# Moving half of the first batch's v1 and v2 projections from the attention stage into the triangle stage, with another word order there

## The chip, the cores and the metric

The kernel runs on one core of one Trainium2 chip. The metric is the time of one execution on the device in microseconds (us); three runs of the kernel before gave 3804.72, 3806.33 and 3807.19 us, so its median is 3806.33 us. Everything is in float32. In what follows PE is the matrix engine, DVE the vector engine, ACT the scalar engine, POOL the GpSimd engine and SP the engine whose queue issues most of the transfers.

## The reference, cut to what matters

Two layers run one after the other on an input x of shape (4, 64, 64, 256): four batches of 4096 tokens with 256 channels. Layer 0 is plain attention over the 4096 tokens of a batch. Layer 1 is a "triangle" attention on the 64 x 64 grid of the same batch, followed by a small MLP.

```python
# layer 0, per batch, t = 4096 tokens
f, g, v = xt @ Wf, xt @ Wg, xt @ Wh            # 32, 32 and 128 channels
beta = softmax(g @ f.T, axis=-1)               # 4096 x 4096
y = xt + (beta @ v) @ Wo + bo                  # the input of layer 1

# layer 1, per batch, H = 8 heads of d_k = 32, N = 64
q, k, v1, v2 = y @ Wq, y @ Wk, y @ Wv1, y @ Wv2
scores = einsum('bilhd,bljhd->biljh', q, k) / sqrt(d_k)
att = softmax(scores, axis=2)                  # over l
out = einsum('biljh,bilhd,bljhd->bijhd', att, v1, v2)
h = layer_norm(y + out @ Wo)
out = layer_norm(relu(h @ W1 + b1) @ W2 + b2 + h)
```

The four projections q, k, v1 and v2 are all made from y, the result of layer 0. The heads are worked on in pairs: pair 0 and pair 1 use channels 0 to 127 of q, k, v1 and v2, pair 2 and pair 3 use channels 128 to 255.

## The kernel before, in the parts that the change touches

The program goes through the batches one by one. For each batch there is an attention stage (`layer0`) and then a triangle stage. Work of other batches that does not depend on the stage is woven into the triangle stages: the first one (`first_layer1`) carries the "front" of batches 1 to 3 (turning x, and making f, g and v of layer 0), the later ones carry the last part (output projection, norms, MLP) of the batch before.

The attention stage goes over eight blocks of 512 queries (`qb`), each in eight groups `k`. A group makes scores, exponentials and weighted values; between the groups stand the projections of the block before, from a table `parts`:

```python
def values(g): ...                             # L469: 4 matmuls of 128x512, o += v.T e
def scores(g): ...                             # L447: 4 matmuls of 128x512; ACT makes e = exp(s)

def proj(qb, name, m, ps=None, st=None, queue=nc.sync):     # q, k or v2; half m of the channels
    ps = pb("proj") if ps is None else ps
    for cc in range(2):
        nc.tensor.matmul(ps, w[:, cc, rows], y(qb, cc), start=(cc == 0), stop=(cc == 1))   # L526
    ...                                        # ACT copies it to st, a transfer stores it to DRAM

def proj1(qb, m, ps=None, st=None, queue=nc.sync):          # v1: all channels of half m of the tokens
    for n in range(2):
        for cc in range(2):
            nc.tensor.matmul(                  # L551, 128x256 each
                ps[:, ts(n, C)], y(qb, cc)[:, ts(m * 2 + n, P)], wv1_sb[:, cc, :],
                start=(cc == 0), stop=(cc == 1),
            )
    ...

parts = [
    [norm, bounds],
    [output],
    [lambda qb: proj(qb, "q", 0)],
    [lambda qb: proj(qb, "k", 0), lambda qb: proj(qb, "v2", 0)],
    [lambda qb: proj1(qb, 0)],
    [lambda qb: proj1(qb, 1), lambda qb: proj(qb, "q", 1)],
    [lambda qb: proj(qb, "k", 1)],
    [lambda qb: proj(qb, "v2", 1)],
]
...
for g in range(8 * NQB):
    ...
    if qb > 0 and not (qb == last and k >= 6):
        for part in parts[k]:
            part(qb - 1)
# ... then a tail: the projections of the last block, the scores of pair 0,
# and the first sums, weights and transposes of the triangle stage
```

The triangle stage has 32 steps, eight for each pair of heads. In each step eight products R = att x v2 of 128x2048 are made, `npool` of them on POOL (three, and two in every fourth step of the first batch) and the others on DVE; PE then contracts each with v1 in four matmuls:

```python
def product(self, step, m):                    # L849
    ...                                        # R: 3 buffers on DVE, Rp: 2 buffers on POOL
    eng.tensor_tensor(R, src.unsqueeze(1).to_broadcast([P, D, N]), v2[:, h], ALU.mult)

def accumulate(self, step, m):                 # L859
    for c in range(4):
        nc.tensor.matmul(acc[32 * c : 32 * c + 32, n % 2, :], w[:, n, c, 16 * h : 16 * h + 32], R[...], ...)
```

The front of a later batch comes in 24 pieces `s` (eight blocks for each of three batches). A piece reads 512 tokens of x into one buffer `xin`, turns them on PE, and the next piece is loaded into the same buffer once the turning is through:

```python
def load(self, s):                             # L329, buffer of its own: tag "hid", bufs=1
    self.x = work.tile([P, 4, C], F32, tag="hid", name="xin", bufs=1)
    nc.sync.dma_start(out=self.x, in_=xf[...])
def turned(self, s, cc): ...                   # word P: 4 transposes (L336)
def taken(self, s, cc): ...                    # word C: ACT copy, store
def values(self, s): ...                       # word v: 8 matmuls of 128x128 (L348); word u: copy, store
def factors(self, s): ...                      # word g: 16 matmuls with 32 columns (L239); word a: copy, store
```

The order of all this is a written list of words, `ORDER0`. It is gone through once for each period of four steps; `R23/1` is product 3 of step 2 of the period before, `A` an accumulation, `T` a taking of the sums, `S`, `W`, `t`, `c`, `V` the preparation of a step, `sp` and `e` the scores of the next pair. Every period had three front pieces:

```python
for period in range(NSTEP // 4 + 3):
    for word, late in words_of(ORDER0):
        i, last = period - late, int(word[-1])
        ...
        elif word[0] in "RATSWVtc":
            step_word(word[0], 4 * i + int(word[1]), last)
        else:
            front_word(word[0], 3 * i + int(word[1]), last)
```

Of the kernel before, what the change touches and what calls it, by code (L numbers as in the profile page):

```python
# [10 lines left out]
F32 = mybir.dt.float32  # L11
# [5 lines left out]
P = 128  # L17
# [3 lines left out]
N = 64  # L21
# [26 lines left out]

ORDER0 = """
    A22/1 t3/1 R23/1 V3/1 W0 A26/1 A21/1 g2/1 A23/1 A25/1 R24/1 T20/1 sp1/1 A24/1 S2 S3 c3/1 t0 R27/1
    v1/1 R31/1 R33/1 a2/1 A27/1 e11/1 e10/1 R30/1 A33/1 A31/1 R32/1 v2/1 u1/1 R37/1 P01 T21/1 A37/1
    A30/1 C01 S1 R35/1 c0 R36/1 A32/1 R34/1 P00 A35/1 A36/1 C00 g0 V0 R01 A34/1 u2/1 T30/1 R00 W1 R05
    T31/1 A05 R06 v0 A00 A01 V1 R03 R02 A03 t1 a0 c1 R04 u0 A06 R13 P11 R07 P10 A02 A07 R15 W2 R12 A04
    T00 C11 T01 sp0 R16 t2 e01 R10 c2 A12 P21 e00 R11 C10 S0/-1 A15 W3 A13 A16 C21 P20 A10 R17 R14 V2
    A11 A14 A17 R26 g1 R25 R20 T11 T10 a1 R22 R21 A20 C20
""".split()


# [1 line left out]
def attention_then_triangle_kernel(  # L62
# [23 lines left out]
    def pb(name):  # L86
        return psB.tile([P, 512], F32, tag="b", name=name)
# [303 lines left out]
                nc.sync.dma_start(out=F.yT[1], in_=d["x"][P : 2 * P, :])  # L391


    def layer0(b, F, safe, rest):
        yT, gT, fT = F.yT, F.gT, F.fT
        if safe:
            F.reduced()

# [122 lines left out]
        def proj(qb, name, m, ps=None, st=None, queue=nc.sync):  # L521
# [19 lines left out]
            else:  # L541
# [2 lines left out]
                    in_=st.rearrange("p (l j) -> p l j", j=N),  # L544
                )

        def proj1(qb, m, ps=None, st=None, queue=nc.sync):
            ps = pb("v1p") if ps is None else ps
            for n in range(2):
                for cc in range(2):  # L550
                    nc.tensor.matmul(  # L551
                        ps[:, ts(n, C)], y(qb, cc)[:, ts(m * 2 + n, P)], wv1_sb[:, cc, :],
                        start=(cc == 0), stop=(cc == 1),
                    )
# [9 lines left out]
        def proj_qk(qk, st):  # L564
# [33 lines left out]
            [lambda qb: proj(qb, "k", 1)],  # L598
            [lambda qb: proj(qb, "v2", 1)],
        ]  # L600
        last = NQB - 1
        scores(0)
        for g in range(8 * NQB):
            qb, k = divmod(g, 8)
            if b == 0 and not safe:
                for load in later[3 * g : 3 * g + 3]:
                    load()
                if g == 6:
                    fold_bias()
                if g == 20:  # L610
                    add_b2()
            if safe and k == 0 and qb + 1 < NQB:
                mx, todo = pieces(qb + 1)
                for qc, t in todo:
                    max_piece(qc, t, mx)
                row[qb + 1] = max_row(mx)
            if g + 1 < 8 * NQB:
                scores(g + 1)
            values(g)

            if qb > 0 and not (qb == last and k >= 6):
                for part in parts[k]:
                    part(qb - 1)
            if qb == last and k == 3:
                L.fetch_v1(0)
                L.fetch_v1(1)
            if qb == last and k == 5:
                if b > 0:
                    rest.load(NP * (b - 1))
                L.fetch_qk(0, True)  # L630
# [27 lines left out]
        def values1(m):  # L658
            proj1(last, m, None, stage[1][:, 1 + m, :], nc.scalar)
# [20 lines left out]
        hidden(0)  # L680
        score(3)
# [19 lines left out]
    class Layer1:  # L701
# [22 lines left out]
        def fetch_v2(self, pair, part=None):  # L724
            if part != 1:
                self.v2[pair] = big.tile([P, 2, D, N], F32, tag="v2", name="v2", bufs=2)
            v2 = self.v2[pair].rearrange("p h d j -> p (h d j)")
            l0, l1 = ((0, 56), (56, 64))[part] if part is not None else (0, 64)
# [419 lines left out]

    def step_words(L, fetched, stored):
        made, taken, sps = {}, {}, {}

        def do(w, step, m):
            if not 0 <= step < NSTEP:
                return
            if w == "R":
                if step not in made:
                    made[step] = 0
                    L.begin(step)  # L1160
                L.product(step, m)
                made[step] += 1
                if made[step] == 8:
                    if step == 1:
                        L.fetch_v2(1)
                    if step in (NIG - 1, 2 * NIG - 1):
# [36 lines left out]

        L.fetch_v1(2)
        return do, scores, take_scores
# [6 lines left out]
    def first_layer1(L, ahead, F):  # L1212
        turned = {}
        ahead.load(0)

        def fetched(step):
            if 24 <= step < 31:
                ahead.fetch(F, 1, step)

        step_word, scores, take_scores = step_words(L, fetched, lambda step: None)  # L1220

        def front_word(w, s, cc):
            if not 0 <= s < ahead.n:
                return
            if w == "P":
                ahead.turned(s, cc)
                turned[s] = turned.get(s, 0) + 1
                if turned[s] == 2:
                    ahead.load(s + 1)
                    if s + 1 == ahead.n:  # L1230
                        ahead.fetch(F, 1, 31)
            elif w == "C":
                ahead.taken(s, cc)
            elif w == "v":
                ahead.values(s)
            elif w == "u":
                ahead.valued(s)
            elif w == "g":
                ahead.factors(s)
            elif w == "a":  # L1240
                ahead.factored(s)

        for period in range(NSTEP // 4 + 3):
            for word, late in words_of(ORDER0):
                i, last = period - late, int(word[-1])
                if word[0:2] == "sp":
                    if i >= 0:
                        if i == last == 0:
                            scores(0)
                            for half in range(2):  # L1250
                                take_scores(0, half)
                        scores(2 * i + 1 + last)
                elif word[0] == "e":
                    if i >= 0:
                        take_scores(2 * i + 1 + int(word[1]), last)
# [178 lines left out]
```

## Time and profile before

| what | value |
|---|---|
| median of three runs | 3806.33 us |
| span of the profiled run | 3803.8 us |
| PE busy over the span | 97% |
| DVE, ACT, POOL busy over the span | 69%, 51%, 47% |
| mean granted PE clock | 0.990 |
| queue that SP, DVE and ACT transfers use: share of 16 engines | 29.2% |

The shares over the whole span mix stages. A stage is read from a stretch of the trace instead: in the first batch the attention stage lies at about 40 to 459 us, its tail at 459 to 497 us, the first triangle stage at 497 to 925 us, and the attention stage of the second batch begins at 925 us. A row of the profile names the line, the engine, the tiles (written on the left of the arrow, read on the right), how often, the busy time, the mean of one, and the idle time of the engine just before, with what ended it. The profile counts two PE instructions for most of the float32 matmuls written in the program.

### The profile page before, as it was taken

The numbers are of one execution on the slowest core, as the hardware profiler recorded it, in microseconds if no ns is written. First come the engines' busy times: TensorE is split into PE (matmuls) and PEld (weight loads), VectorE is DVE, ScalarE is ACT, GpSimd is POOL, SyncE is SP. The second block draws the span as 40 slices with busy tenths as digits, with TensorE's granted clock in tenths as the row PEclk, the third lists the DMA queues.
The fourth block names the chain that finished last, engine by engine and source line by source line (L and its number), as shares of the span: only waits on it lengthen the run. The fifth ranks groups of instructions, "written<-read, shape, count | busy, mean of one in ns | idle before, by whom it ended". The sixth has DMA issues, their size and how long they took to land.

```text
span 3803.8 us, 60205 instructions
## 1 busy us (share of the span) xinstructions
PE 3679.2 (97%) x23498; PEld 1797.3 (47%) x23498; DVE 2641.2 (69%) x2050; ACT 1931.2 (51%) x4257; POOL 1804.3 (47%) x930
## 2 busy tenths in 40 slices
PE   9999988998999999999999999999999999999997
PEld 5444444433444455554344455555344445555476
DVE  4444479997544459999544548999754445999976
ACT  3333355554333357776333346766533335677654
POOL 4000079996000049999200008999600004999944
PEclk9999999999999999999999999999999999999999
DMA  4111355544111164323111143343211116431221
GB/s 118 54 50 49 95 142 143 148 124 142 36 47 53 50 151 93 88 55 94 62 47 50 50 124 89 84 95 70 92 41 48 50 54 149 95 89 48 69 62 51
DMA packets 439750, 309.44 MB, mean 81 GB/s; under 512 B 299360, under 2 KB 404576, under 8 KB 432160
## 3 DMA queue, kind: packets, MB, share of 16 engines
q1 hardware_dynamic: 419952, 291.12, 29.2%
q10 hardware_dynamic: 16240, 8.59, 0.8%
q0 software_dynamic: 3264, 5.78, 0.7%
q8 instruction: 188, 3.08, 0.4%
q14 instruction: 106, 0.87, 0.1%
HBM read 165.88 MB, written 139.46 MB: 80 GB/s over the span
## 4 chain that ended last, share of the span: by engine, by line
PE 80%; POOL 5%; DMA 4%; DVE 4%; issue 4%; ACT 2%; SPq 1%; ACTq 0%; POOLq 0%; DVEq 0%
PE o L469 24%; PE acc L859 17%; PE proj L526 8%; PE s L447 7%; PE mp L1042 5%; PE zp L1062 5%; POOL Rp L849 4%; PE v1p L551 3%; PE sp L747 3%; DMA xin<-in_x_dram 2%; DVE R L849 2%; PE hp L918 2%; PE y L511 2%; PE att L801 1%; PE den L486 1%
## 5 line engine op out<-in xcount | busy, mean ns | idle before, releaser
L849 POOL TENSOR_TENSOR Rp<-attP,v 128x2048 f32<-128x2048 f32 x328 | 1490.1, 4576 | 448.4 <-DMA qk<-k 326.0
L849 DVE TENSOR_TENSOR R<-att,v 128x2048 f32<-128x2048 f32 x696 | 1546.9, 2274 | 103.5 <-PE acc L859 69.6
L476 DVE TENSOR_TENSOR esum<-esum,e 128x2048 f32<-128x2048 f32 x224 | 512.8, 2289 | 583.2 <-ACT e L458 579.6
L859 PE MATMUL acc<-R,wsel 128*32 128x512 f32 x5568 | 701.1, 602 | 24.6 <-DVE R L849 13.2
L458 ACT ACTIVATE e<-s 128x1024 f32<-128x1024 f32 x512 | 496.5, 1021 | 403.5 <-PE s L447 388.5
L970 POOL TENSOR_SCALAR nt<-mv 128x4 f32<-128x4 f32 (+1 forms) x51 | 9.9, 193 | 1287.2 <-DVE mv L935 1276.3
L469 PE MATMUL o<-e,vlo 128*128 128x512 f32 x1024 | 473.7, 605 | 0.0
L469 PE MATMUL o<-e,vhi 128*128 128x512 f32 x1024 | 472.6, 605 | 0.0
L859 PE MATMUL acc<-Rp,wsel 128*32 128x512 f32 x2624 | 351.0, 607 | 10.2 <-POOL Rp L849 9.2
L869 ACT COPY ao<-acc 128x1024 f32<-128x1024 f32 x256 | 254.1, 1020 | 186.7 <-PE acc L859 125.5
L859 PEld LDWEIGHTS acc<-R,wsel 128*32 128x32 f32 x5568 | 154.3, 110 | 356.5 <-issue 272.3
L469 PEld LDWEIGHTS o<-e,vlo 128*128 128x128 f32 x1024 | 184.0, 189 | 280.8 <-issue 280.8
L469 PEld LDWEIGHTS o<-e,vhi 128*128 128x128 f32 x1024 | 184.3, 189 | 279.7 <-issue 279.7
L447 PE MATMUL s<-gT,fT 32*128 32x512 f32 x2048 | 302.2, 640 | 4.7 <-ACT e L458 4.3
L784 ACT ACTIVATE es<-S,rd 128x64 f32<-128x64 f32 x1024 | 257.8, 336 | 2.1 <-ACT stage L538 1.3
L488 DVE RECIPROCAL rec<-den 128x512 f32<-128x512 f32 x32 | 107.5, 3358 | 215.6 <-PE den L486 215.6
L1062 PE MATMUL zp<-w,hid 128*128 128x256 f32 x1024 | 245.9, 385 | 7.5 <-ACT hid L1051 7.5
L1042 PE MATMUL mp<-hT,w 128*128 128x256 f32 x1024 | 249.5, 389 | 0.7 <-ACT hT L1014 0.7
L1042 PEld LDWEIGHTS mp<-hT,w 128*128 128x128 f32 x1024 | 186.5, 190 | 101.4 <-ACT attP L809 36.9
L1062 PEld LDWEIGHTS zp<-w,hid 128*128 128x128 f32 x1024 | 185.3, 190 | 72.1 <-issue 29.3
L538 ACT COPY st<-proj 128x512 f32<-128x512 f32 x104 | 60.9, 585 | 293.2 <-issue 165.9
L447 PEld LDWEIGHTS s<-gT,fT 32*128 32x128 f32 x2048 | 82.9, 182 | 193.6 <-issue 174.8
(166 smaller groups left out, 3833.6 us busy)
## 6 DMA issues: line engine op xcount, KB each, us to landing
v<-v2d SPq DMA_DIRECT2D x24, 1024.0 KB, 12.4
v1c<-v1d SPq DMA_DIRECT2D x128, 128.0 KB, 2.8
aT<-ao SPq DMA_DIRECT2D x1024, 16.0 KB, 1.9
A<-aT SPq DMA_DIRECT2D x256, 64.0 KB, 2.1
out_dram<-z SPq DMA_DIRECT2D x63, 256.0 KB, 2.5
y<-yT SPq DMA_DIRECT2D x56, 256.0 KB, 2.1
q<-st SPq DMA_DIRECT2D x56, 256.0 KB, 2.6
v1d<-st SPq DMA_DIRECT2D x56, 256.0 KB, 2.2
```

The costliest lines, as they stand in the source:

```text
L447: nc.tensor.matmul(s_ps[r // 2][:, r % 2, :], fT[rows, tt, ts(n, P)], gT[rows, ts(qb, QB)], start=True, stop=not safe,)
L458: nc.scalar.activation(e[g][:, 2 * j : 2 * j + 2, :], s_ps[j], AF.Exp)
L469: nc.tensor.matmul(o_ps[qb], F.v[tt][:, r * 4 + n, :], es[:, r, :], start=(k == 0 and r == 0), stop=(k == 7 and r == 3),)
L476: nc.vector.tensor_tensor(esum[qb], esum[qb], es, ALU.add)
L526: nc.tensor.matmul(ps, w[:, cc, rows], y(qb, cc), start=(cc == 0), stop=(cc == 1))
L551: nc.tensor.matmul(ps[:, ts(n, C)], y(qb, cc)[:, ts(m * 2 + n, P)], wv1_sb[:, cc, :], start=(cc == 0), stop=(cc == 1),)
L784: nc.scalar.mul(e[:, i, :], rows[:, i, :], rec[:, i : i + 1])
L849: eng.tensor_tensor(R, src.unsqueeze(1).to_broadcast([P, D, N]), v2[:, h], ALU.mult)
L859: nc.tensor.matmul(acc[32 * c : 32 * c + 32, n % 2, :], w[:, n, c, 16 * h : 16 * h + 32], R[:, ts(c, 8), :].rearrange("p d j -> p (d j)"), ...
L869: nc.scalar.copy(self.ao[step][:, ts(np, 2)].rearrange("p k d j -> p k (d j)"), self.acc[step][np])
L1042: nc.tensor.matmul(self.mp[:, fc % 2, :], w1_sb[:, cc, ts(fc, P)], self.hT[tt][:, cc, :], start=(cc == 0), stop=(cc == 1),)
L1062: nc.tensor.matmul(zp[:, n, :], self.hid[tt][:, fc, ts(n, P)], w2_sb[:, fc, :], start=(fc == 0), stop=(fc == 3 and tt not in self.hT2),)
```

## The change

One half of v2 and of v1 of batch 0, the channels 128 to 255 which only the pairs 2 and 3 read, is no longer made in the attention stage. It is made in the first triangle stage, in eight blocks, by a class `Late` with four new words: `m` makes v2 of a block and `n` copies and stores it, `o` makes v1 and `p` copies and stores it. `Late` reads y back from DRAM into two buffers. v2 of pair 2 is fetched from DRAM by rows as they get stored. To make room, the front pieces are spread two to a period over the first four periods and four to a period over the last four. ORDER0 is a new list throughout. The aim is to take PE work out of a stage in which PE is the busiest engine and to put it into one in which PE has idle time.

```diff
 ORDER0 = """
-    A22/1 t3/1 R23/1 V3/1 W0 A26/1 A21/1 g2/1 A23/1 A25/1 R24/1 T20/1 sp1/1 A24/1 S2 S3 c3/1 t0 R27/1
...  (five more lines)
+    A21/2 g1/2 S3/1 W1/1 A27/2 A23/2 A26/2 a1/2 V3/2 A24/2 P31/2 C21/2 R32/2 m1/2 T20/2 c3/2 P30/2 C31/2
+    t0/1 v2/2 n1/2 R25/2 A25/2 R33/2 sp0/1 T21/2 A32/2 C30/2 R34/2 R36/2 R30/2 A33/2 e00/1 u2/2 e01/1
+    o1/2 R31/2 g2/2 P00/1 c0/1 R37/2 A34/2 A36/2 A30/2 A31/2 A37/2 V0/1 R35/2 C00/1 T30/2 t1/1 R00/1
+    p1/2 P01/1 a2/2 C01/1 A35/2 R03/1 T31/2 A00/1 R02/1 g0/1 a0/1 R05/1 R07/1 A05/1 A03/1 v3/2 R06/1
+    u3/2 m0/1 S2/1 W2/1 c1/1 v0/1 V1/1 R01/1 A02/1 n0/1 R04/1 A07/1 A01/1 A04/1 R12/1 P11/1 u0/1 P10/1
...  (three more lines)
 """.split()
...
+    def v1_half(ps, ys, m):
+        for n in range(4):
+            for cc in range(2):
+                nc.tensor.matmul(
+                    ps[:, ts(n, P)], ys[cc][:, ts(n, P)], wv1_sb[:, cc, ts(m, P)],
+                    start=(cc == 0), stop=(cc == 1),
+                )
...
+    class Late:
...
+        def load(self, q):
+            self.y = []
+            for cc, tag in enumerate(("A", "yc")):
+                t = work.tile([P, 512], F32, tag=tag, name="yb", bufs=1)
+                nc.sync.dma_start(out=t, in_=self.io["y"][ts(cc, P), ts(q, 512)])
+                self.y.append(t)
...
+        def word(self, w, q):
...
+            if w == "m":
+                ps = self.ps[w, q] = pb("v2p")
+                for cc in range(2):
+                    nc.tensor.matmul(ps, wv2_sb[:, cc, ts(1, P)], self.y[cc], start=(cc == 0), stop=(cc == 1))
+                self.made(q)
+            elif w == "o":
+                ps = self.ps[w, q] = pb("v1p")
+                v1_half(ps, self.y, 1)
+                self.made(q)
+            else:
+                st = work.tile([P, 512], F32, tag="sx", name="sx", bufs=1)
...                                            # n: copy, store v2, fetch its rows; p: copy, store v1
+        def fetch(self):
+            if self.room and self.fetched < self.stored:
+                self.L.fetch_rows(2, 8 * self.fetched, 8 * self.stored)
+                self.fetched = self.stored
...  (layer0)
+        late = b == 0
...
+        if late:
+            parts[3] = [lambda qb: proj(qb, "k", 0)]
+            parts[4] = [lambda qb: proj(qb, "v2", 0)]
+            parts[5] = [proj1_half]
+            parts[6] = [lambda qb: proj(qb, "q", 1)]
+            parts[7] = [lambda qb: proj(qb, "k", 1)]
...
-            if qb > 0 and not (qb == last and k >= 6):
+            if qb > 0 and not (qb == last and k >= 6 + late):
...
-        proj(last - 1, "v2", 1, None, stage[0][:, 1, :])
+        if not late:
+            proj(last - 1, "v2", 1, None, stage[0][:, 1, :])
...
-        values1(0)
+        if late:
+            proj1_half(last, stage[1][:, 1, :], nc.scalar)
+        else:
+            values1(0)
...
-        values1(1)
+        if not late:
+            values1(1)
...
-        proj(last, "v2", 1, None, stage[2][:, 1, :], nc.scalar)
+        if not late:
+            proj(last, "v2", 1, None, stage[2][:, 1, :], nc.scalar)
...  (first_layer1; "sp" and "e" count the scores from 2 * i now, without a special first one)
+                elif word[0] in "mnop":
+                    if 0 <= i < 4:
+                        own.word(word[0], 2 * i + last)
+                elif 0 <= i < 4 and int(word[1]) < 2:
+                    front_word(word[0], 2 * i + int(word[1]), last)
+                elif 4 <= i < 8:
+                    front_word(word[0], 4 * i - 8 + int(word[1]), last)
-                else:
-                    front_word(word[0], 3 * i + int(word[1]), last)
```

More of the change, by code (lines that the diff above doesn't have):

```diff
@@ L51 @@
 ORDER0 = """
-    A22/1 t3/1 R23/1 V3/1 W0 A26/1 A21/1 g2/1 A23/1 A25/1 R24/1 T20/1 sp1/1 A24/1 S2 S3 c3/1 t0 R27/1
[L53 to L57, printed above, removed]
+    A21/2 g1/2 S3/1 W1/1 A27/2 A23/2 A26/2 a1/2 V3/2 A24/2 P31/2 C21/2 R32/2 m1/2 T20/2 c3/2 P30/2 C31/2
[3 more added lines that the diff above has]
+    u3/2 m0/1 S2/1 W2/1 c1/1 v0/1 V1/1 R01/1 A02/1 n0/1 R04/1 A07/1 A01/1 A04/1 R12/1 P11/1 u0/1 P10/1
+    A06/1 T00/1 sp1/1 C11/1 T01/1 R13/1 R15/1 R14/1 A13/1 e10/1 e11/1 t2/1 C10/1 R10/1 A12/1 R17/1 V2/1
+    A15/1 A14/1 A10/1 R16/1 R11/1 S0 R22/1 W3/1 g3/2 c2/1 W0 A17/1 R27/1 A11/1 v1/1 R20/1 a3/2 u1/1 o0/1
+    p0/1 S1 R21/1 T10/1 P20/1 t3/1 P21/1 A16/1 T11/1 C20/1 A20/1 R23/1 A22/1 R24/1 R26/1
 """.split()
@@ L391, in fetch, with store_v1 @@
                 nc.sync.dma_start(out=F.yT[1], in_=d["x"][P : 2 * P, :])
+    def v1_half(ps, ys, m):
[5 more added lines that the diff above has]
+                )
+    def store_v1(io, q, m, st, queue=nc.sync):
+        queue.dma_start(
+            out=io["v1"][ts(q, 512), ts(m, P)].rearrange("(n p) c -> p n c", p=P),
+            in_=st.rearrange("p (n c) -> p n c", n=4),
+        )
@@ new lines, in attention_then_triangle_kernel, with __init__, made @@
+    class Late:
+        def __init__(self, L):
+            self.L, self.io, self.q = L, L.io, None
+            self.ps, self.stored, self.fetched, self.room = {}, 0, 0, False
+            self.load(0)
+        def load(self, q):
[4 more added lines that the diff above has]
+                self.y.append(t)
+            self.used = 0
+        def made(self, q):
+            self.used += 1
+            if self.used == 2 and q + 1 < NQB:
+                self.load(q + 1)
+        def word(self, w, q):
+            if not 0 <= q < NQB:
+                return
+            if w == "m":
[9 more added lines that the diff above has]
+                st = work.tile([P, 512], F32, tag="sx", name="sx", bufs=1)
+                if w == "n":
+                    nc.scalar.copy(st, self.ps.pop(("m", q)))
+                    nc.sync.dma_start(
+                        out=self.io["v2"][ts(q, 8), ts(1, P), :].rearrange("l c j -> c l j"),
+                        in_=st.rearrange("p (l j) -> p l j", j=N),
+                    )
+                    self.stored = q + 1
+                    self.fetch()
+                else:
+                    nc.scalar.copy(st, self.ps.pop(("o", q)))
+                    store_v1(self.io, q, 1, st)
+        def fetch(self):
+            if self.room and self.fetched < self.stored:
+                self.L.fetch_rows(2, 8 * self.fetched, 8 * self.stored)
+                self.fetched = self.stored
@@ L545, in proj, with proj1_half @@
                 )
+        def proj1_half(qb, st=None, queue=nc.sync):
+            st, ps = staged(st), pb("v1p")
+            v1_half(ps, [y(qb, cc) for cc in range(2)], 0)
+            nc.scalar.copy(st, ps)
+            store_v1(io, qb, 0, st, queue)
         def proj1(qb, m, ps=None, st=None, queue=nc.sync):
@@ L670, in layer0 @@
             rest.affine_a(t0)
-        values1(0)
+        if late:
+            proj1_half(last, stage[1][:, 1, :], nc.scalar)
+        else:
+            values1(0)
         score(1)
@@ L726, in fetch_v2, with fetch_rows @@
                 self.v2[pair] = big.tile([P, 2, D, N], F32, tag="v2", name="v2", bufs=2)
+            if part != 2:
+                self.fetch_rows(pair, *(((0, 56), (56, 64))[part] if part is not None else (0, 64)))
+        def fetch_rows(self, pair, l0, l1):
             v2 = self.v2[pair].rearrange("p h d j -> p (h d j)")
-            l0, l1 = ((0, 56), (56, 64))[part] if part is not None else (0, 64)
             for i2 in range(2):
@@ L1145, in alone, with step_words @@
                 closed(n, known[n])
-    def step_words(L, fetched, stored):
+    def step_words(L, fetched, stored, late=None):
         made, taken, sps = {}, {}, {}
@@ L1165, in do @@
                         L.fetch_v2(1)
-                    if step in (NIG - 1, 2 * NIG - 1):
+                    if step == NIG - 1 and late is not None:
+                        L.fetch_v2(2, 2)
+                        late.room = True
+                        late.fetch()
+                    elif step in (NIG - 1, 2 * NIG - 1):
                         L.fetch_v2((step + 1) // NIG + 1)
@@ L1218, in fetched @@
                 ahead.fetch(F, 1, step)
-        step_word, scores, take_scores = step_words(L, fetched, lambda step: None)
+        own = Late(L)
+        step_word, scores, take_scores = step_words(L, fetched, lambda step: None, own)
         def front_word(w, s, cc):
@@ L1247, in first_layer1 @@
                     if i >= 0:
[L1248 to L1252, printed above, removed]
+                        scores(2 * i + last)
                 elif word[0] == "e":
                     if i >= 0:
-                        take_scores(2 * i + 1 + int(word[1]), last)
+                        take_scores(2 * i + int(word[1]), last)
                 elif word[0] in "RATSWVtc":
                     step_word(word[0], 4 * i + int(word[1]), last)
-                else:
-                    front_word(word[0], 3 * i + int(word[1]), last)
+                elif word[0] in "mnop":
[5 more added lines that the diff above has]
+                    front_word(word[0], 4 * i - 8 + int(word[1]), last)
         ahead.fetch(F, 1, NSTEP)
```

## The prediction, made before the changed kernel had run

> **What bounds the kernel now.** The whole-span shares (PE 97%) mix stages, so I first cut the span by windows into the stages of the first batch. Columns: length, then the busy time of PE, of its weight loads, of DVE, ACT and POOL, each with the number of instructions, the granted PE clock, the DMA share and GB/s.
>
> ```profile
> 40.00:459.00 419.00, 416.01 (x1353) 174.08 (x1352) 202.39 (x126) 156.38 (x183) 35.86 (x59) 1.00 0.21 60
> 459.00:497.00 38.00, 29.00 (x324) 16.79 (x324) 9.68 (x15) 16.70 (x32) 7.13 (x2) 0.91 0.79 189
> 497.00:925.00 428.00, 386.61 (x4284) 177.79 (x4284) 389.86 (x223) 232.62 (x610) 392.36 (x87) 0.96 0.52 138
> ```
>
> To be seen: in the attention stage (first line) PE is busy 416 of 419 us and everything else under half, so it is PE's stage and each us of PE work costs a us. In the triangle stage (third line) PE, DVE and POOL are all at 90 to 92%, none is full, and the PE clock is 0.96. So no engine bounds it throughout; something stops all three in turn. The waits of PE in that stretch say what:
>
> ```profile
> PE tp L336 <- DMA xin<-in_x_dram: 25.2, 7, 6.5
> PE acc L859 <- POOL Rp L849: 6.7, 14, 0.8
> PE acc L859 <- DVE R L849: 6.7, 7, 1.9
> ```
>
> (total us, times, longest.) The turning of x waits for its load, seven times, up to 6.5 us. PE runs in order, so nothing behind it goes on. The groups of DVE and POOL show the echo: their idle time ends when PE has released a product buffer.
>
> ```profile
> L849 DVE TENSOR_TENSOR R<-att,v 128x2048 f32<-128x2048 f32 x167 | 370.5, 2278 | 39.5 <-PE acc L859 35.0 <-DMA q<-stage 3.9 <-ACT attP L809 0.2
> L849 POOL TENSOR_TENSOR Rp<-attP,v 128x2048 f32<-128x2048 f32 x87 | 395.0, 4588 | 33.3 <-PE acc L859 32.7 <-POOL Rp L849 0.6
> ```
>
> Last I took the timeline of PE for the price of each piece of work. A single matmul's duration overlaps its neighbour's, so I use distances between starts:
>
> ```profile
> 428.26 1.88 PE L526 MATMUL proj<-yT,wk 128*128 128x512 f32 x4
> 429.98 1.88 PE L526 MATMUL proj<-yT,wv 128*128 128x512 f32 x4
> 431.79 1.14 PE L447 MATMUL s<-gT,fT 32*128 32x512 f32 x8
> 432.86 3.70 PE L469 MATMUL o<-e,vhi 128*128 128x512 f32 x8
> 436.40 1.89 PE L551 MATMUL v1p<-wv,yT 128*128 128x256 f32 x8
> 438.22 1.14 PE L447 MATMUL s<-gT,fT 32*128 32x512 f32 x8
> ...
> 911.48 2.05 PE L348 MATMUL vp<-wh,xT 128*128 128x128 f32 x16
> 913.58 1.06 PE L859 MATMUL acc<-Rp,wsel 128*32 128x512 f32 x8
> ```
>
> One v2 half of a block is 431.79 - 429.98 = 1.8 us, one v1 call 438.22 - 436.40 = 1.8 us (two calls to a block), and eight matmuls of 128x128 (the shape that the new v1 half has; vp, L348) some 2.0 to 2.1 us.
>
> **What the Trainium skill says.** "Perfetto Trace Analysis", section Identifying the Most-Contended Engine, warns that PE's busy share is no measure of distance to its limit, as pipelined matmuls overlap in the trace; the rows above agree (1.88 us of duration, 1.72 to 1.81 us from start to start), which is why I count by starts. The same page, section Optimization Strategy, recommends interleaving regimes whose busiest engine differs; that is what this change does, and the first two windows against the third show such regimes. "TensorE: Matmul & The Clock Gate", Part 1, says PE's clock is halved after about 3.4 us of idling and takes a similar time to come back. The trace fits: after a wait of 5.37 us the eight transposes of the next piece take 1.94 us, undisturbed ones 1.09 us, and the stage has a clock of 0.96 against 1.00 in attention. "DMA: Bandwidth & Descriptors", section Issuing engines are not separate DMA queues, says all transfers share the same 16 engines and interleave; the xin load lands after 6.5 us at the median, but the one issued at 607.36 us, right behind two 1 MB fetches of v2, held PE until 621.4 us, 14 us later.
>
> **The change, part by part.**
>
> *Out of the attention stage.* For each of the eight blocks v2's upper half goes (1.8 us) and the two v1 calls (3.6 us) become one of eight 128x128 matmuls (2.0 us): 1.8 + 1.6 = 3.4 us a block. In the loop lie six of the v2 halves (the last two are in the tail) and seven of the v1: 6 x 1.8 + 7 x 1.6 = 22 us, all of it on the path, as PE has no waits there. In the tail 2 x 1.8 + 1.6 = 5.2 us of PE work goes, but PE is busy only 29 of 38 us there and the first products wait for v2 by way of DRAM. I count 3 us. Sum: -25 us.
>
> *Into the triangle stage.* Eight times (1.8 + 2.0) = +30 us of PE, and sixteen ACT copies of 0.59 us, 9.4 us on an engine busy 233 of 428 us, which cost nothing. The work PE has there now, by starts: 256 accumulations x 0.88 = 225; weights' transposes 31 x 0.59 = 18; scores 12 x 1.85 = 22; 24 fronts of 1.0 (turning) + 0.9 (factors) + 2.0 (values) = 94. Together 359 us; then 389 us. DVE has 167 products 2.21 us apart plus 28 x 0.83 us of sums: 392 us. POOL has 89 products (two before the window) 4.55 us apart: 405 us. So PE comes up to the level of DVE, both a little under POOL, and POOL's 405 us is the floor of the stage. It takes 435 us now, from POOL's first product at 489.9 to 925.
>
> *The fronts.* A period is 53.5 us. With three pieces, the shortest stretch between the end of one turning and the next one in the old list (P10 to P21) held three or four accumulations, one score, one transpose and the rest of a front: about 6 us of PE work, less than the 6.5 us that the load takes. By the new list, half of the periods have two pieces, with P01 to P11 some 11.6 us apart (eight accumulations 7.0, factors 0.9, v2 1.8, values 2.0) and the other distances longer. In the four-piece periods the shortest is P21 to P31, eight accumulations and a front's factors, 8 us, and P01 to P11 9.9 us. All are over 6.5 us. In addition v2 of pair 2 is fetched by rows, in place of one 2 MB burst. I expect the 18.7 us of xin waits within the stage (25.2 less the 6.5 at its entry) to fall to about 5, from the one burst left (pair 3 is fetched in a four-piece period), and part of the slow-clock time with them. PE work of a period is then 28 + 2.4 + 3.7 + 15.6 = 50 us, beside 51 for DVE and 50 for POOL: with three engines this close, in order and with two or three product buffers, some new short waits must come. I put them at 4 us. So the triangle stage gets 14 - 4 = 10 us shorter.
>
> *Sum.* -25 - 10 = -35 us: 3806 - 35 = 3771 us; for small losses in the seam to the second batch (values and factors of the last front piece now stand behind the last accumulation, 3 us of PE) I say 3773 us.
>
> **The rivals.**
>
> *A: the stage is full, and the work only moves.* If the triangle stage now was limited by the coupling of three engines and not by xin, +30 us of PE lengthens it by up to 30 us, and the change gains nothing (3800 to 3810 us). For it: in the periods without an xin wait DVE and POOL are already busy 52 to 54 of 54 us. Against it: in those periods PE has only about 46 us of work, and in the triangle stage of the second batch, from 1425 to 1725 us, PE is busy 50 of 50 us in each slice with DVE and POOL at 48. So a list of words can hold three engines near full. A partial case, with the stage as long as before, gives 3806 - 25 = 3781 us.
>
> *B: the transfers become the wait.* Reading y back (4 MB), v1 stored in runs of 512 bytes, and stores of v2 followed at once by their fetch on the same SP queue could hold up the xin loads and the stores of the sums. For it: the DMA share is 0.52 here, and SP already waits in order on ACT. Against it: 8 MB of added traffic beside some 59 MB (138 GB/s x 428 us) is one seventh more, and y has 7 us or more of PE work to land in. This would put back the 14 us of xin gain or more: 3785 to 3795 us.
>
> *C: everything fits.* The triangle stage gets near POOL's floor, 405 / 0.97 = 417 us, 18 us shorter: 3806 - 25 - 18 = 3763 us, or a few us lower if the tail gains all its 5.2 us.
>
> **Range and chances.** The 22 us of the attention loop are nearly sure. The spread comes from the triangle stage: 18 us shorter (C) to 14 us longer (between A and B). That gives 3761 to 3795 us; with a margin below for a better clock, 3755 to 3795 us. To be faster by over 2% the time must be under 3730 us, 76 us less: that is more than the attention saving and all of the stage's idle time together (22 + 5 + 30), so 1%. Slower by over 2% needs the triangle stage 100 us longer, a broken list: 1%. Within 2%: 98%.
>
> **What would show it.** The seven loop blocks should be 22 us shorter together; if less, ACT or DVE limits attention. In the triangle stage the xin wait of PE should be under 12 us with its entry, the clock above 0.96, DVE and POOL busy 94% or more. A stage longer than 430 us with waits of PE on R and Rp speaks for A; waits on yb, xin or v2 from DRAM for B. The later batches should not change; if they do, my sum is wrong in a place I did not look at.

## The result, and the profile after

The changed kernel takes 3782.64 us (median of four runs, 3778.28 to 3790.86) against 3806.4 us before (3804.72 to 3807.19): a ratio of 0.9941, with a 95% interval of 0.9923 to 0.9958. The change gains about 24 us; 33 were forecast. The profiled runs span 3803.8 and 3782.1 us.

Stages by windows, the changed kernel (columns as before; the stages begin and end earlier now):

```profile
40.00:435.00 395.00, 393.40 (x1324) 161.35 (x1324) 201.00 (x125) 148.72 (x170) 35.95 (x59) 1.00 0.19 54
435.00:471.00 36.00, 25.55 (x370) 15.78 (x374) 10.27 (x14) 17.18 (x38) 6.98 (x2) 0.88 0.76 185
471.00:901.50 430.50, 398.85 (x4404) 199.32 (x4397) 391.54 (x225) 244.02 (x617) 393.11 (x87) 0.98 0.59 155
```

Attention is as full of PE as before, only shorter. The triangle stage has more PE work and a better clock (0.98 for 0.96), but DVE and POOL still only work 391 and 393 of 430 us. To compare two kernels I take marks that both have, from the timeline of PE, in us:

| mark | before | after | gained so far |
|---|---|---|---|
| last sum of the denominators of batch 1 (attention loop) | 454.41 | 431.80 | 22.6 |
| first transpose of the triangle stage | 487.67 | 461.82 | 25.9 |
| first scores of the second batch's attention | 925.00 | 901.48 | 23.5 |
| end of the span | 3803.8 | 3782.1 | 21.7 |

So the whole gain was there when the triangle stage began, and the stage went from 437.3 to 439.7 us.

The waits of PE in that stage, the changed kernel:

```profile
PE vp L352 <- ACT gf L251: 5.6, 2, 2.9
PE sp L844 <- DMA qk<-k: 5.6, 2, 4.6
PE v2p L439 <- DMA yb<-y: 5.3, 3, 4.5
PE tp L340 <- ACT gf L251: 4.1, 2, 2.4
PE tp L340 <- DMA xin<-in_x_dram: 3.9, 2, 2.8
PE vp L352 <- ACT xT L345: 3.0, 4, 1.0
```

The xin wait, 25.2 us before, is 3.9. In its place stand five others: the first scores wait for q and k at the entry, the late v2 for y, and the front's matmuls for a PSUM buffer that ACT empties late (the two rows with gf) or for ACT's copy of the turned x (xT).

All of PE's idle time in the stage fell by 10 us, from 47.7 to 37.7, and its busy time rose by 12 us, from 389.6 to 402.0, though the late matmuls alone take 31 us by distances between starts: the other matmuls together took less time than before, beside the better clock. Yet the stage is no shorter. The groups of DVE and POOL show the same:

```profile
L946 DVE TENSOR_TENSOR R<-att,v 128x2048 f32<-128x2048 f32 x168 | 374.1, 2276 | 40.0 <-PE acc L956 26.6 <-ACT attP L906 9.6 <-DMA q<-stage 3.8
L946 POOL TENSOR_TENSOR Rp<-attP,v 128x2048 f32<-128x2048 f32 x88 | 400.1, 4582 | 357.1 <-ACT attP L906 329.6 <-PE acc L956 17.4 <-ACT va L359 6.0
```

DVE's idle time is 40.0 us, as before (39.5), although POOL waits less on PE (17.4 for 32.7 us; the 329.6 is the attention stage before). To see when it idles I counted 21 DVE products at a time (a period's share) from the timeline and took the distance from start to start (the last has 20), in us:

| products | 1st | 2nd | 3rd | 4th | 5th | 6th | 7th | 8th |
|---|---|---|---|---|---|---|---|---|
| before | 65.5 | 50.6 | 57.4 | 50.4 | 56.3 | 49.5 | 52.5 | 49.5 |
| after | 60.0 | 51.3 | 51.1 | 57.8 | 55.7 | 51.2 | 53.5 | 50.0 |

The first three together are 11 us shorter, and two of them stand at DVE's own work of a period (21 x 2.21 + 4 x 0.83 = 50 us, and a few short waits). The other five are 10 us longer. The theory to test:

- **N (new waits).** Three things at definite places took back what the removed xin waits gave: the load of y around the change of pairs in the fourth period, the xin load behind the fetch of v2 of pair 3 in the fifth, and the one staging buffer of the factors in the periods with four fronts.
- **A (full stage).** The stage pays for the 30 us of PE work as such.
- **A2.** The transfers at the change of pairs hold the stage, and a wait that is taken away there comes back as another.

The load of y, PE and SP queue, the changed kernel:

```profile
652.76 1.95 PE L401 MATMUL v1p<-wv,yb 128*128 128x128 f32 x16
...
668.76 3.78 PE L439 MATMUL v2p<-yb,wv 128*128 128x512 f32 x4 [4.50 <-DMA yb<-y]
```

```profile
644.13 0.49 SPq L812 DMA_DIRECT2D qk<-q  x1
...
647.38 15.02 SPq L975 DMA_DIRECT2D aT<-ao  x8
...
664.35 0.87 SPq L424 DMA_DIRECT2D yb<-y  x2
```

The y buffers are free when the matmuls of 652.76 are through, at about 654.5 us. But the load is issued only at 664.35: ahead of it on SP are eight small stores whose issue took 15.0 us, behind 2 MB of q and k of the next pair. The same eight take 5.0 us elsewhere (at 665.79). PE waits 4.5 us, then works at a granted clock of 0.50 (3.78 us for four instructions that else take 1.98), and DVE idles 7.00 us until 677.58.

### The profile page after: what moved, and what is told of

It reads as the page before. It is cut to its first block, busy times and chain, and to the rows that moved or that the text cites. A ratio compares the mean times of both kernels' runs of the same rounds, so it can differ in the third digit from the quotient of the medians.

```text
span 3782.1 us, 60452 instructions
## 1 busy us (share of the span) xinstructions
PE 3667.2 (97%) x23626; PEld 1805.3 (48%) x23626; DVE 2642.4 (70%) x2050; ACT 1936.3 (51%) x4257; POOL 1806.1 (48%) x930
## 4 chain that ended last, share of the span: by engine, by line
PE 82%; POOL 7%; DMA 4%; DVE 3%; issue 2%; ACT 2%; SPq 1%; ACTq 0%; POOLq 0%; DVEq 0%
PE o L544 24%; PE acc L956 17%; PE proj L601 8%; PE s L522 7%; POOL Rp L946 5%; PE zp L1159 5%; PE mp L1139 5%; PE sp L844 3%; PE v1p L633 2%; PE hp L1015 2%; DMA qk<-k 2%; PE y L586 1%; DVE R L946 1%; PE att L898 1%; DMA xin<-in_x_dram 1%
## 5 line engine op out<-in xcount | busy, mean ns | idle before, releaser
L613 ACT COPY st<-proj 128x512 f32<-128x512 f32 x98 | 57.4, 586 | 288.3 <-PE proj L601 160.2
L854 ACT ACTIVATE S<-sp 128x512 f32<-128x512 f32 x128 | 129.9, 1119 | 93.7 <-PE sp L844 93.7
```

Source lines behind the costliest of these rows:

```text
L854: nc.scalar.activation(self.S[pair][:, :, l0 : l0 + 8].rearrange("p i l -> p l i"), sp[:, lh], AF.Copy if self.safe else AF.Exp,)
```

## The experiments

The time of each is the median of its own runs; intervals are of the ratio to the kernel before. "Stage" is from the first transpose to the first scores of the second batch in its one profiled run. One warning: the triangle and attention stages of the later batches, whose program text is the same in all kernels here, took between 2213.9 and 2221.2 us in the profiled runs (from the end of the stage to the last denominators of batch 4). A difference of some us in a total can therefore be chance; I read the stage first. The stage has a spread too, as single periods show whose text is the same: the first took 58.5 to 60.2 us in the changed kernel and in five of the runs below (e4, e6, e7, e9, e10), the eighth 50.0 in the changed kernel and 52.9 in e5. So a stage that differs by 3 us proves little; a period that comes out alike in several runs says more.

**The new order without the move** (e1).

```diff
-        late = b == 0
+        late = False
-        own = Late(L)          # and the words m, n, o, p do nothing
```

> The new word list and the uneven spread of the fronts, without the move: attention makes all of v1 and v2 as before. Theory N (new waits: the triangle stage kept its 437 to 440 us because one late load of y, the single staging buffer of the factors in the four-front periods and one late xin load took the place of the old xin waits): without the y loads the triangle stage should be some 8 to 10 us shorter than in the changed kernel, about 430 us from the first transposes to the attention of the second batch, and the whole 3806 - 7 = about 3799 us. Rival A (the stage is full and the moved 30 us of PE work is what it pays for): without this work the stage falls by 20 us or more, to 420 us or less, and the whole to about 3788 us.

3800.97 us, ratio 0.9989 (0.998 to 0.9998), stage 434.9 us. Nearer to N's 430 us than to A's 420: without the moved work the stage is only 4.8 us shorter than with it. It also says what the new list and spread alone are worth: 2.4 us of stage. The fourth period, with the change of pairs in it, takes 51.5 us here, for 57.8 in the changed kernel.

**The move without its PE work** (e2). This kernel leaves out the late matmuls of v1 and v2, so its output is not the reference's.

```diff
             if w == "m":
-                ps = self.ps[w, q] = pb("v2p")
-                ... matmuls
+                self.made(q)   # "o" likewise; n and p copy a weight tile in place of the result
```

> The changed kernel with the matmuls of the late v1 and v2 halves left out (30 us of PE work; wrong data is stored in their place, all copies, loads and stores stay). Attention is that of the changed kernel. Theory N: the periods 1 to 3 stay at 51.2 us, the DVE's own work, and only the wait for y (7 us of DVE idle in the period of the change of pairs) goes: 3773 to 3777 us. Rival A: the stage gets 20 to 30 us shorter: 3753 to 3763 us.

3779.95 us (3775.28 to 3780.9), ratio 0.9934 (0.9917 to 0.995), stage 434.5 us. The stage as a window, the changed kernel first, then this one:

```profile
461.80:901.50 439.70, 402.00 (x4451) 201.54 (x4452) 394.81 (x226) 248.65 (x636) 400.09 (x88) 0.98 0.60 158
463.60:898.10 434.50, 380.84 (x4288) 181.60 (x4288) 394.83 (x226) 248.06 (x636) 399.84 (x88) 0.96 0.59 159
```

**A falls**: leaving out 31 us of matmuls shortens the stage by 5 us, not by 20 to 30, and the second and third period stay at 51.4 and 50.7. PE's busy time falls by only 21 us, as the clock goes back to 0.96 and the other matmuls take 10 us longer. N's time is slightly missed, and for a reason: y is no longer waited for, but the periods around the change of pairs still take 55.8 and 56.7 us. DVE now waits there, in this kernel, for the stores:

```profile
681.26 6.68 DVE L941 TENSOR_TENSOR R<-att,v 128x2048 f32<-128x2048 f32 x3 [4.01 <-DMA aT<-ao]
...
703.81 4.49 DVE L941 TENSOR_TENSOR R<-att,v 128x2048 f32<-128x2048 f32 x2 [3.93 <-PE acc L951]
```

That is the first sign of A2. Set beside e1 it says more. Both kernels lack the late matmuls; e2 has the late loads of y, copies, stores and row fetches, and its fourth period takes 55.8 us for 51.5. The fetch of q and k for the next pair is in both. So the change of pairs alone does not cost the fourth period its time; most of it comes with the transfers and copies of the late work. The eight stores behind that fetch show it on SP, in e1:

```profile
673.69 9.36 SPq L975 DMA_DIRECT2D aT<-ao  x8
```

They are issued 1.5 us after the last fetch, as in the changed kernel, and take 9.4 us for its 15.0.

**The move with the old list** (e3).

```diff
-    ... the new list, 2 and 4 fronts to a period
+    ... t1 a0 c1 R04 u0 m0 A06 R13 P11 R07 n0 P10 ... C21 o0 P20 A10 p0 ...
+    ... a1 m1 R22 R21 A20 C20 n1   and   u1/1 o1/1 R37/1 p1/1 P01 ...   (the old list, 3 fronts)
```

> The move alone: the old word list with three fronts to each period, and the new words m, n, o, p put in at free places by hand. Theory N: the old xin waits stay (some 19 us within the stage) and 31 us of PE work come on top, in the first four periods, where PE then has 54 us of work against 51 of DVE: stage 445 to 455 us, the whole 3787 to 3800 us; so most of what the new list is worth, 5 to 15 us, shows here. Rival A: the same stage as in the changed kernel within 3 us, 3780 to 3785 us, as the work is the same.

3838.31 us, ratio 1.0087 (1.007 to 1.0103), stage 492.2 us: worse than either theory said, and slower than the kernel before. Its periods are 73, 66, 68, 70 and 59 us while the late work lasts, then 50 to 52. The waits of PE in its stage:

```profile
PE tp L338 <- DMA xin<-in_x_dram: 33.9, 6, 8.5
PE v2p L437 <- DMA yb<-y: 11.7, 2, 6.7
PE acc L954 <- DVE R L944: 7.8, 9, 1.9
```

I put the new words in by hand, so this is one bad placing and no bound on what the old list could carry. But the same work with the written list and the spread of the change takes 52 us less. PE's waits for xin and y alone are 45.6 us here and 9.2 there: whether the move pays at all depends on the order and the spread.

**An even spread** (e8), with the new list and the move.

```diff
-                elif 0 <= i < 4 and int(word[1]) < 2: ...      # two to a period, then four
-                elif 4 <= i < 8: ...
+                elif int(word[1]) < 3:
+                    front_word(word[0], 3 * i + int(word[1]), last)
```

> The changed kernel with three front pieces to each period in all eight periods, as before the change (and the word p1/2 moved ahead of P00/1, so that the two PSUM buffers suffice). PE then has some 54 us of work in the first four periods and 46 us in the last four, against 50 and 50. Theory N: the first four periods take 54 to 57 us in place of 51.2, the last four get at most 2 us shorter each: 5 to 15 us slower than the changed kernel, 3788 to 3798 us. Rival: PE's work does not bind at all, the spread is worth nothing: within 3 us of the changed kernel.

3795.8 us, ratio 0.9976 (0.9967 to 0.9984), stage 450.9 us. The time is the one that N said. The first five periods take 62.4, 56.9, 59.8, 57.8 and 60.7, where N said 54 to 57 for four of them, the last three 50.3, 50.3 and 46.0. The mechanism is at most partly the one expected: besides PE's sum of work, ACT stood for the one factor buffer, and this run does not part the two. In this kernel:

```profile
ACT gf L251 <- DMA ahf<-gf: 41.7, 7, 13.5
```

**The factor buffer** (e4, then e7 and e9). In the changed kernel ACT and SP show the wait:

```profile
801.16 0.37 ACT L251 ACTIVATE gf<-gf,bias_g 128x128 f32<-128x128 f32 x1 [6.81 <-DMA ahf<-gf]
```

```profile
794.04 0.61 SPq L370 DMA_DIRECT2D ahg<-gf  x1
794.74 0.43 SPq L370 DMA_DIRECT2D ahf<-gf  x1
```

The factors of one piece are stored from 794.0 us, behind a fetch of 512 KB and an xin load; those of the next piece can't be written before 801.2. PE's next values then wait 2.73 us for the PSUM buffer. First try:

```diff
-            t = work.tile([P, 2, C], F32, tag="h", name="gf", bufs=1)
+            t = work.tile([P, 2, C], F32, tag="sx" if s >= 8 and s % 2 else "h", name="gf", bufs=1)
```

> The changed kernel with a second staging buffer for the factors of every other front piece of the second half (the buffer that the late v1 and v2 copies no longer use). Theory N: the ACT waits for the store of the factors (16.7 us) go, and with them the 2 to 3 us that DVE and POOL lose in each of the last periods: 4 to 7 us faster than the changed kernel, 3776 to 3779 us. Rival A: no difference.

3780.64 us, ratio 0.9936 (0.992 to 0.9953), stage 441.6 us, the ACT wait 15.4 us for 16.7. Nothing, and the trace shows why: pieces 2 and 0 follow each other within 10 us in the list and are both even, so they still shared one buffer. So turns by the order of use:

```diff
+            self.turn = s >= 8 and not getattr(self, "turn", False)
+            t = work.tile([P, 2, C], F32, tag="sx" if self.turn else "h", name="gf", bufs=1)
```

> As the earlier run with a second factor buffer, which did nothing since the two pieces that follow each other within 10 us (a2 and a0 of the list) still had the same buffer: now the two buffers take turns by the order of use. Theory N: the ACT waits for the store of the factors (16.7 us) fall below 4 us and the last three periods lose 2 to 5 us together: 3777 to 3781 us. Rival A2: the waits go but the time stays, as POOL (50 us of work to a period) and DVE (51 us) take 51 us or more anyway: within 1 us of the changed kernel.

3781.0 us, ratio 0.9939 (0.9922 to 0.9956), stage 437.2 us. The wait for the store is gone and the last two periods fall from 53.5 and 50.0 to 52.8 and 46.4, but the fifth grows from 55.7 to 59.0. The borrowed buffer is still being stored from by the last late v1, in this kernel:

```profile
ACT gf L251 <- DMA v1d<-sx: 10.3, 1, 10.3
```

With the turns from piece 10 on (`s >= 10`):

> The factor buffers take turns as in the run before, but only from front piece 10 on, so that the second buffer is no longer shared with the last copies of the late v1 (that cost a wait of 10.3 us on ACT and a period of 59.0 in place of 55.7 us). Theory N: the stage falls by the 3 us of that wait to 434 us, the last three periods stay at those of the run before: 3775 to 3779 us. Rival A2 (the transfers at the change of pairs hold the stage, whatever buffer is doubled): within 1 us of the run before, 3780 to 3782 us.

3776.52 us (3775.52 to 3780.12), ratio 0.9921 (0.9907 to 0.9934), stage 434.4 us: that wait is gone too, the fifth period is at 56.0 again. N is right about this buffer. The stage is 5.3 us shorter, but 1.5 of that lie in the first period, whose text is the same; the last two periods give 4.0 us. The eighth takes 46.4 to 46.9 us in all five runs with the turns (e7, e9 to e12), for 50.0 in the changed kernel.

**The transfers at the change of pairs** (e5, e6, e10, e11). First, y on another queue, behind the copy of v1:

```diff
                     store_v1(self.io, q, 1, st)
+                    if q + 1 < NQB:
+                        self.load(q + 1, nc.scalar)     # in place of nc.sync, after the second use
```

> The changed kernel with the loads of y for the late halves issued on the ACT queue, right after the copy of v1 of the block before, in place of the SP queue, where the one for the last block stood behind 15 us of stores. Theory N (the single late y load costs 6 to 7 us of DVE and POOL idle at the change of pairs): the wait of PE for y goes, the stage gets 4 to 7 us shorter than the changed kernel's 439.7 us, the whole 3776 to 3779 us. Rival A2 (the run without the moved PE work still had 55.8 us and 56.7 us in the two periods around the change of pairs, so the transfers of that moment hold the stage anyway, through xin or the stores): the y wait goes but another takes its place, 0 to 2 us.

3795.06 us (3787.2 to 3799.87), ratio 0.997 (0.996 to 0.998), stage 450.5 us: both theories missed, it is 11 us worse. y's wait fell only from 5.3 to 3.5 us, and ACT could not empty the sums, since the stores of the sums were late, in this kernel:

```profile
ACT ao L960 <- DMA aT<-ao: 17.6, 3, 11.6
```

The fourth period takes 64.4 us. Why the stores were held so long by half a MB on the other queue I have not shown.

Second, v2 of pair 3 in pieces:

```diff
-                    elif step in (NIG - 1, 2 * NIG - 1):
-                        L.fetch_v2((step + 1) // NIG + 1)
+                    # at steps 15 to 21: 8 rows of each half of v2 of pair 3 (16 at step 21)
+                        L.fetch_rows(3, 8 * k, 8 * k + 8)
```

> The changed kernel with v2 of pair 3 fetched in seven pieces over seven steps in place of one 2 MB fetch. Theory N: the xin load behind that fetch lands in 7 us in place of 13, its wait of 2.8 us goes, and the period with 55.7 us gets 2 to 4 us shorter: 3778 to 3781 us. Rival A2: no difference.

3781.64 us, ratio 0.9939 (0.9923 to 0.9956), stage 442.1 us. PE's xin wait in the stage falls from 3.9 to 0.8 us and the fifth period from 55.7 to 52.5, as N says; then the 6th to 8th grow from 154.7 to 160.8 us together, with longer waits for the factor buffer (19.8 for 16.7 us). Of these 6 us 2.5 lie in the eighth, which took 52.9 in e4 and e5 too and can be chance. So the two cures belong together:

> The same with v2 of pair 3 fetched in seven pieces, which took the xin wait away before (2.9 to 0.8 us) but gave the gain back through longer waits for the store of the factors. Theory N: with two factor buffers those waits are gone, so the 3 us stay gained: 3772 to 3777 us. Rival A2: the pieces delay other stores, within 1 us of the run without them.

**3771.53 us** (3770.24 to 3775.67), ratio 0.9909 (0.9896 to 0.9923), stage 432.9 us: the fastest version here, 11 us below the changed kernel. Its stage accounts for 6.8 us of the 11. The rest lies before the stage (1.3) and in the later batches, where the text is the same, and I can't tell it from chance. Against e9 the fifth period gives 3.6 us, but the stage only 1.6. The fifth period is 52.5, the last two 54.4 and 46.9; only the entry (59.2) and the fourth period (57.5) are still long.

Third, to get y ahead of q and k, the words o0 and p0 moved forward (on e9):

```diff
-    ... A07/1 A01/1 A04/1 R12/1 P11/1 u0/1 P10/1 ... u1/1 o0/1 p0/1 S1
+    ... A07/1 o0/1 A01/1 A04/1 u0/1 R12/1 P11/1 p0/1 P10/1 ... u1/1 S1
```

> Factor buffers in turns from piece 10 on, and the words o0 and p0 moved forward by some 60 places, ahead of the fetch of q and k of the next pair, so that y of the next block is asked for before that 2 MB fetch and the stores behind it. Theory N (the y load is late because it stands behind the fetch): the wait for y at the change of pairs goes, the period of 57 us becomes 52 to 54 us: 3771 to 3776 us. Rival A2 (bandwidth at that moment is short, as y on the ACT queue showed, where the stores of the sums waited instead): y is no longer waited for, but the stage stays within 2 us.

3786.19 us, ratio 0.9947 (0.9934 to 0.9961), stage 446.7 us. PE no longer waits for y, which is asked for at 651.97 us, but the stores stand as long as before, in this kernel:

```profile
660.10 15.12 SPq L976 DMA_DIRECT2D aT<-ao  x8
```

and the fourth and fifth period still take 56.8 and 57.8 us. For these two A2 is right: y is no longer waited for, and nothing is gained. For the stage both theories missed, as it is 12 us longer than e9's: the new order also costs the first three periods (61.3, 53.8 and 57.3 for 58.5, 51.4 and 51.1).

**The entry** (e12, on e10).

```diff
-                    if i >= 0:
-                        scores(2 * i + last)
+                    if i == 0 and last == 1:         # the first scores of pair 1 just ahead of the second
+                        scores(0); take_scores(0, 0); take_scores(0, 1)
+                    if i >= 0 and (i, last) != (0, 0):
+                        scores(2 * i + last)
```

> The run with turns and v2 in pieces, and the first scores of pair 1, which hold PE at the entry of the triangle stage for 5.5 us until q and k have come from DRAM, made half a period later, just ahead of the second ones. Theory N (a word that waits on DRAM at the head of PE's queue costs the stage its wait): the first 21 DVE products take 57 in place of 59 us, 3768 to 3771 us; not the full 5.5 us, since the turning of x then waits for its own load, issued behind. Rival A2 (the entry is held by transfers altogether): PE waits as long on the next load, no difference.

3781.49 us, ratio 0.9937 (0.9924 to 0.9951), stage 438.3 us. Where PE waited 5.5 us for q and k, it now waits for xin, in this kernel:

```profile
470.80 1.09 PE L340 MATMUL tp<-ident,xin 128*128 128x128 f32 x4 [8.37 <-DMA xin<-in_x_dram]
```

PE starts its front at the same 470 us, and the first period grows from 59.2 to 64.4. The 1.9 us of scores and their ACT copies now come later, in a fuller place; that this is what the 5 us are is not shown. A2 is right about the wait, N's "costs its wait" falls for the entry, and the time is worse than either said.

## Why the prediction was right or wrong

- **Attention, -25 us: right.** Each block gains 3.39 us (3.4 said), the loop gives 22.6 (22), the tail 3.2 (3). The new v1 half costs 1.8 to 2.0 us, as vp did.
- **The xin waits: right in kind.** PE waits 3.9 us for xin in the stage (5 said), 2.78 of it at the place named, behind the fetch of v2 of pair 3, and 1.15 in the seventh period. The 50 us of PE work to a period were right too: in the second and third period, 51.2 us long, PE is busy 50.0 and 50.1, and e2, without the late matmuls, is no more than 0.4 us faster there. (One count was off: POOL has 88 products, not 89, so the floor is 400 us, not 405.)
- **"I put them at 4 us", the new short waits: wrong, and the step that failed.** Beside xin, PE's list has 5.6 us for q and k at the entry, where xin was waited for before and would have been again, 5.3 for y, and 12.7 for ACT (5.6 + 4.1 + 3.0). The change of -10 us for the stage came out as +2.4. The runs place most of these 12 us. The single factor buffer was not looked at: with four fronts to a period two pieces come within 10 us of each other, and a second buffer gives 4 us back in the last two periods (e9). The one fetch of v2 of pair 3 costs the fifth period 3.2 us (e6, and the same in e10). And the late work's own transfers and copies cost the fourth period most of the 6 us between e1 and the changed kernel, as e2 shows with 55.8 us. There y "has 7 us or more of PE work to land in" was counted from the matmuls that free its buffers; the load stood on SP for 10 us before its issue. That y alone is the cost is not shown: e11 took its wait away and gained nothing.
- **The rivals.** A was rightly put low: e2 takes 31 us of PE work away for 5 us of stage. Its partial case, the stage as long as before, named the time almost to the us (3781), but by luck, since PE's work is not what held the stage. B, transfers as the wait, was nearest in kind: it named reading y back, the stores of the sums and the shared SP queue. It said 3785 to 3795 and so overrated the cost. What e1, e2, e5 and e11 show is that with the late transfers something is late around the change of pairs whichever load is put first. C, all fits, did not come about: 439.7 us of stage, not 417.
- **The range held** because the attention term carries it: that term alone gives 3806 - 26 = 3780 us. The stage was off by 12 us, more than all it was to gain.
- Left open: why the eight stores of the sums take 15 us to issue there. The fetch of q and k ahead of them does not account for it alone (9.4 us in e1). In the changed kernel a store of v2 and a fetch of its rows, 256 KB each, also stand just ahead, and in e2 and e11, which have them too, the stores take 13.9 and 15.1 us; a run without these two alone was not made. Left open too: the 1.8 us that the later batches took longer in the profiled run, which is inside their spread.

## What to carry to other kernels

Work moved out of a stage that one engine fills is gained at once, and can be priced by distances between starts; whether the other stage takes it for nothing depends on its order of work, its buffers and the transfers that come with the work, and is not seen from the shares of busy time. Before packing more of a kind of work closely, count the buffers that each piece holds, through the store that frees them, and look at where that store stands in its queue. When three engines are each busy 91 to 93% of the time, price a load from the moment it can be issued, not from the moment its buffer is free.

## What the runs showed of the hardware that I had not expected

Issuing eight stores of 16 KB took 9.4 us in place of 5.0 behind 2 MB of fetches on the same queue (e1), and 15.0 us where a store and a fetch of 256 KB each stood ahead as well (the changed kernel); everything behind them waited for that. Moving the loads of y, 512 KB each, to the ACT queue, where they no longer stand behind stores, made the stage 11 us longer, with ACT waiting 17.6 us for the stores. Adding 31 us of matmuls to a stage raised PE's busy time by only 21 us (e2 against the changed kernel), with a granted clock of 0.98 in place of 0.96. And the same later batches, with the same 12220 PE instructions in the same order, took 2213.9 to 2221.2 us in different kernels.
